# Normalized tokens of 56 tiles: turned by TensorE, or by VectorE and DRAM

## The chip, the core and the metric

The kernel runs on one core of a Trainium2 chip, as one program. A core has a matrix engine (TensorE, PE in the profile, with its weight loads shown apart as PEld), a vector engine (VectorE, DVE), a scalar engine (ScalarE, ACT), a general engine (GpSimd, POOL), and SyncE (SP), which here issues the data transfers. A transfer moves between DRAM and the on-chip memory (SBUF) on 16 DMA engines. TensorE writes its results to a small second memory (PSUM), from which VectorE or ScalarE has to carry them to SBUF. Each engine works through its own list of instructions in order, and waits on semaphores for the others. The metric is the device time of one execution, in microseconds, as the median of several.

## The reference

The input `x` is 2 images of 1024 tokens with 1024 channels, in float32. Four layers follow each other, each with a residual: attention A (32 heads of 32, causal, rotary positions, and ten learned adapter tokens), a feed-forward layer, attention B (8 heads of 16, not causal), and the same feed-forward layer again, with the same weights.

```
x = x + attn_a(layernorm(x), w_attn, w_proj, adapter_wte, gating)
x = x + ffn(layernorm(x), W_base, b_base, W_router, b_router, lora_A, lora_B)
x = x + attn_b(layernorm(x), Wqk_w, Wqk_b, Wv_w, Wv_b, Wo_w, Wo_b)
x = x + ffn(layernorm(x), W_base, b_base, W_router, b_router, lora_A, lora_B)

def ffn(x, ...):
    base = x @ W_base.T + b_base                       # 1024 x 1024
    weights = sparsemax(x @ W_router.T + b_router)     # 8 experts
    h = einsum('bsd,edr->bser', x, lora_A)             # rank 16 each
    return base + einsum('bser,bse,ero->bso', h, weights, lora_B)
```

Each dense layer multiplies normalized tokens by weights and sums over the channels. TensorE sums over the partitions of its operands, so the channels have to lie on the partitions, while a layer norm needs each token's channels together on one partition. Between the two every tile of 128 tokens by 1024 channels has to be turned.

## The kernel before

**Tiles.** A tile is 128 tokens; an image has NT = 8. `layernorm` (L241) leaves `xn`, tokens on partitions; `transposed` (L281) turns it by eight 128x128 transposes on TensorE into PSUM, four to a bank, and `evac` (L229) copies each bank to SBUF, by turns on VectorE and ScalarE. The result is `xnT` in attention A (half an image, 512 tokens) and `xt` elsewhere (one tile, eight blocks of 128 channels).

**Order on TensorE.** The attention loop `attend` (L474) writes down TensorE's instructions round by round, and between them a `Filler` (L49) puts in dense work: generators that yield after each matmul what it costs, at 1.7 ns a column. The list is fixed at build time (`manual_schedule`), and TensorE follows it whatever is late. On VectorE and ScalarE the tile framework orders the instructions. SP's list follows the program from the end of stage A on; before that it is the framework's. In the part that the program orders, a transfer's place on SP is where `sp.dma_start` was called.

**Stage A.** Projections of attention A are computed per group of four heads, by a scheme with seven products in place of eight (`seven`, L669), whose combined token blocks `tt` stream from DRAM through five buffers (`Stream`, L613). Image 0 is turned at once (`half`, L730). Image 1 is normalized early (`normalize_ahead`, L736) and put aside in DRAM as `xnd`; `second` (L746) brings it back a tile at a time, and turns it in pieces between the matmuls of group 7 of image 0 and of the first projection of image 1 (`turn_over`, L767). `xnT` has two buffers, so half an image of image 1 can only be placed when that of image 0 is done with.

**The feed-forward layers.** `ffn` (L1243) is called as `f1(0)`, `f1(1)` (first layer, one image each) and four times as `f2` (second layer, half an image each). It goes in pairs of tiles: `hidden` (L1312) computes the router and the low-rank part (`hp`), then come seven products in the order 1, 6, 2, 7, 5, 4, 3 (`seven_added`, L1069), of four matmuls each. Products 6, 7 and 4 use combined weights, which stream from DRAM tile `tf` into one ring (`qkb_f` and `qkb_s` in the profile), four pieces each, issued in `used` as TensorE frees the places: pieces 3 for product 7 as product 6 goes on, pieces 4 for product 4 during product 7, pieces 2 for the next pair. The next pair's tiles are fetched, normalized and turned during the pair; the transposes stand between matmuls (`also`, L1441), as in

```
turns = {(5, 0): (2, 0), (5, 3): (2, 1), (4, 2): (3, 0), (3, 1): (3, 1)}
```

The first pair of the first `f2` goes without the scheme (`plain`, L1342).

**Attention B.** `project_b` (L1470) does a tile at a time: values `bv`, transposes of the next tile, queries and keys `bq`. `project_b(0)` and the first `hp` of `f1(1)` come before the attention loop of B; `f1(1)`, `project_b(1)` and the first `f2` calls are filler inside it. `project_wo` (L1537) adds the output projection `bo` to reloaded tokens `xo`.

`Dense.prepare` (L1690) runs a generator's first steps early, one `yield None` at a time, so that loads and layer norms are under way when its first matmul comes.

## Time and profile before

| | |
|---|---|
| three runs | 2406.2, 2408.8, 2414.7 us |
| median | 2408.8 us |
| span of the profiled execution, first to last instruction | 2407.9 us |
| TensorE busy | 2351.2 us, 98% |
| VectorE, ScalarE, GpSimd busy | 1437.3, 1100.4, 598.6 us |
| moved by DMA | 274.7 MB, the 16 engines 35% busy |

The profiled execution is known by its span; what lies around it isn't shown, and the median of the runs is 0.9 us above the span. Times in the listings are microseconds from the start of the span, unless marked ns. A line of the timeline gives start, length, engine, source line, operation, written tile, read tile, shapes and how many instructions were merged; TensorE's are pipelined, so one instruction's length is more than the time it holds the engine. SPq marks the issue of a transfer on SP. A group's three durations are minimum, median and maximum in ns. A line of the transfers ends with the size and the median time from issue to landing. A stage's line gives the length, then busy time and count of PE, PEld, DVE, ACT and POOL, the granted TensorE clock, the DMA share and GB/s.

By stage: attention A with its projections fills 0 to 1190 us; the output projection of A reaches 1460; `f1(0)` stands alone from 1460 to 1592 and `project_b(0)` to 1645; then the loop of attention B runs to about 2250, and the last two `f2` calls stand alone to the end.

### The profile page before, as it was taken

Reading aid. Unit: us, or ns where it says so; the run is one execution under the profiler, and the core shown is the slowest. Engines: PE = TensorE matmul, PEld = TensorE weight load, DVE = VectorE, ACT = ScalarE, POOL = GpSimd, SP = SyncE. Lnnn points to the kernel's source line nnn. Section 1 sums busy time; section 2 is a strip of 40 time slices with the busy share of each in tenths; the row PEclk is TensorE's granted clock in tenths of the full one; section 3 lists DMA queues with packets and bytes.
Section 4 is the critical chain, followed back from the end, with each engine's and each line's share of the span. In section 5 each row is a group of like instructions: output and inputs, shape, how many; then the busy total and the mean of one; then the engine's idle time right before and its main releaser. Section 6 shows DMA issues by size and latency. Waiting matters only on the chain.

```text
span 2407.9 us, 60616 instructions
## 1 busy us (share of the span) xinstructions
PE 2351.2 (98%) x25151; PEld 1077.8 (45%) x25151; DVE 1437.3 (60%) x4317; ACT 1100.4 (46%) x2106; POOL 598.6 (25%) x933
## 2 busy tenths in 40 slices
PE   8999999999999999999999999999999999999999
PEld 4435443455354444445433445575333653233454
DVE  6587666666656666666651246566666765664453
ACT  3346665666565666666652001012455546564100
POOL 1432232222323232223211114202111111122332
PEclk9999999999999999999999999999999999999999
DMA  4443433333243333332312575441332302323543
GB/s 151 141 132 111 136 91 132 98 94 107 90 123 103 92 96 106 88 98 77 133 58 71 174 258 174 159 148 60 121 94 91 112 20 80 105 85 101 175 158 122
DMA packets 174772, 274.70 MB, mean 114 GB/s; under 512 B 16416, under 2 KB 76960, under 8 KB 174496
## 3 DMA queue, kind: packets, MB, share of 16 engines
q1 hardware_dynamic: 174496, 270.83, 35.2%
q8 instruction: 197, 3.23, 0.6%
q14 instruction: 79, 0.65, 0.1%
HBM read 215.19 MB, written 55.57 MB: 112 GB/s over the span
## 4 chain that ended last, share of the span: by engine, by line
PE 89%; DVE 6%; ACT 2%; DMA 1%; issue 1%; POOL 0%; SPq 0%; DVEq 0%; POOLq 0%; ACTq 0%
PE st L411 10%; PE sc L339 8%; PE y_A L433 5%; PE y L200 5%; PE y_f L198 4%; PE z_f L198 4%; PE z L200 4%; PE st L409 3%; PE x_f L198 3%; PE x L200 3%; PE y_v L200 3%; PE y_f L200 3%; PE y_B L433 2%; PE x_f L200 2%; PE y_p L198 2%; DVE pr_A L352 2%
## 5 line engine op out<-in xcount | busy, mean ns | idle before, releaser
L523 ACT ACTIVATE pt<-st 128x1024 f32<-128x1024 f32 (+1 forms) x418 | 425.5, 1018 | 605.8 <-PE st L411 463.6
L360 ACT ACTIVATE pr_A<-pr_A,nmax_A 128x896 f32<-128x896 f32 (+7 forms) x512 | 389.9, 765 | 55.1 <-DVE nmax_A L352 54.5
L352 DVE CUSTOM_DVE_ANT_0 pr_A<-sc,mask 128x512 f32<-128x512 f32 (+3 forms) x512 | 251.2, 537 | 190.2 <-PE st L411 90.7
L339 PE MATMUL sc<-kT,qT 32*128 32x512 f32 (+3 forms) x1536 | 326.1, 521 | 4.8 <-POOL qT L851 3.0
L411 PE MATMUL st<-qT,kT 32*128 32x512 f32 (+3 forms) x1536 | 306.4, 486 | 0.0
L352 DVE CUSTOM_DVE_ANT_0 pr_A<-sc,mask,part_A 128x512 f32<-128x512 f32 (+1 forms) x256 | 156.2, 647 | 145.7 <-PE sc L339 95.0
L418 POOL TENSOR_SCALAR_AFFINE_SELECT pt<-pt 128x256 f32<-128x256 f32 x256 | 105.9, 431 | 469.1 <-ACT pt L523 469.1
L239 POOL TENSOR_TENSOR xf<-xf,b_base 128x256 f32<-128x256 f32 x100 | 74.5, 775 | 417.8 <-DVE xn_f L267 261.9
L360 ACT ACTIVATE pr_B<-pr_B,nmax_B 128x1024 f32<-128x1024 f32 x128 | 145.5, 1141 | 36.4 <-DVE nmax_B L352 36.3
L433 PE MATMUL y_A<-pt,v 128*32 128x512 f32 (+3 forms) x1536 | 157.9, 498 | 0.0
L339 PE MATMUL sc<-kq,qk 32*128 32x512 f32 x512 | 146.5, 649 | 4.6 <-DVE nmax_B L352 3.8
L411 PE MATMUL st<-rows_B,kq 32*128 32x512 f32 x512 | 145.8, 646 | 2.4 <-ACT pt L523 1.7
L411 PEld LDWEIGHTS st<-qT,kT 32*128 32x128 f32 x1536 | 133.6, 185 | 16.3 <-issue 11.3
L409 PE MATMUL st<-rows_A,ones 3*128 3x512 bf16 (+3 forms) x768 | 127.8, 329 | 5.6 <-DVE nmax_A L352 5.0
L352 DVE CUSTOM_DVE_ANT_0 pr_B<-sc,zeros,part_B 128x512 f32<-128x512 f32 x128 | 91.0, 747 | 59.3 <-PE sc L339 59.3
L409 PEld LDWEIGHTS <-ones 3*128 3x128 bf16 x768 | 36.9, 91 | 194.7 <-issue 187.3
L339 PEld LDWEIGHTS sc<-kT,qT 32*128 32x128 f32 x1536 | 113.0, 184 | 18.3 <-POOL qT L851 5.0
L352 DVE CUSTOM_DVE_ANT_0 pr_B<-sc,zeros 128x512 f32<-128x512 f32 x128 | 83.2, 687 | 60.4 <-PE sc L339 60.2
L850 POOL TENSOR_TENSOR qr<-qr,sin 128x256 f32<-128x256 f32 x64 | 61.3, 957 | 220.9 <-DVE qr L846 213.9
L360 ACT ACTIVATION_READ_ACCUMULATOR pr_A<-pr_A,nmax_A 128x1 f32 x512 | 97.2, 190 | 0.0
L200 PE MATMUL y<-tt,wqk 128*32 128x512 f32 x768 | 92.6, 594 | 0.0
L433 PEld LDWEIGHTS y_A<-pt,v 128*32 128x32 f32 x1536 | 33.7, 108 | 118.2 <-issue 109.9
(424 smaller groups left out, 4232.8 us busy)
## 6 DMA issues: line engine op xcount, KB each, us to landing
tt<-td SPq DMA_DIRECT2D x252, 256.0 KB, 2.9
qkb_f<-tf SPq DMA_DIRECT2D x96, 256.0 KB, 3.0
qkb_s<-tf SPq DMA_DIRECT2D x84, 256.0 KB, 2.9
wqk<-in_w_attnT SPq DMA_DIRECT2D x32, 512.0 KB, 5.2
xf<-x SPq DMA_DIRECT2D x25, 512.0 KB, 3.7
xa<-in_x SPq DMA_DIRECT2D x16, 512.0 KB, 6.0
wv<-in_w_attnT SPq DMA_DIRECT2D x8, 1024.0 KB, 5.3
yd<-ys SPq DMA_DIRECT2D x32, 256.0 KB, 2.7
```

Of the source, the lines that this page charges most:

```text
L198: return pe.matmul(out, lhsT=lhsT, rhs=rhs, start=start, stop=stop, skip_group_check=True)
L200: pe.matmul(out[i : i + 32], lhsT=lhsT[:, i : i + 32], rhs=rhs, start=start, stop=stop, skip_group_check=True)
L239: pool.tensor_add(dst[:, i : i + 2 * P], a[:, i : i + 2 * P], b[:, i : i + 2 * P])
L339: yield w * COL, lambda: pe.matmul(dst[:, o : o + w], lhsT=self.qt[rows, qc : qc + P], rhs=self.kt[rows, c0 : c0 + w], start=True, stop=True)
L352: minimum[0] = dve.tensor_tensor_reduce(pr[:, c0 : c0 + w], sc[:, i, o : o + w], m, -self.scale, BIG if c0 == 0 else self.part[:, col], AL ...
L360: tc.keep_in_program_order(act.activation(pr[:, :nk], pr[:, :nk], AF.Exp, bias=self.nmax[:, col], scale=-1.0, accum_out=self.sums[:, col]))
L409: yield w * COL / 4, lambda: pe.matmul(dst[:, o : o + w], lhsT=of["ones"][three, :], rhs=self.rows[three, off : off + w], start=True, stop ...
L411: yield w * COL, lambda: pe.matmul(dst[:, o : o + w], lhsT=self.kt[rows, kb * P : (kb + 1) * P], rhs=rhs, start=self.extra, stop=True)
L418: pool.affine_select(out=dg, in_=dg, compare_op=ALU.is_ge, fill=0.0, base=0, pattern=[[0, 2], [1, P]], channel_multiplier=-1)
L433: pe.matmul(self.y[32 * h : 32 * h + 32, off : off + w], lhsT=self.value(h, kb), rhs=pt[h // 2][:, h % 2, o : o + w], start=self.opens, st ...
L523: act.activation(pt[:, :, low_:wide_], st[:, :, low_:wide_], AF.Exp, scale=ts[0][0].scale)
L850: pool.tensor_mul(qr[:, hs], qr[:, hs], sin[:, cols][:, hs])
```

## The change

All 56 tiles that went through TensorE on the dense stages' way, save image 0's eight in stage A, are turned otherwise: eight of image 1 in stage A, 32 in the feed-forward layers, 16 in `project_b`. A normalized tile is turned by one VectorE instruction in blocks of 32x32 (each block in its place), written to a DRAM tile, and read back by 16 transfers, one for each pair of 32 tokens and 32 of the partitions, in runs of 32 floats (128 bytes). The 16 reads land in the places that the evictions of PSUM wrote.

```diff
+    def turned_out(pl, tag, xn, dst, name, bufs=None):
+        d = pl.tile([P, 4, NC, 32], F32, tag=tag, name=f"d_{name}", **({"bufs": bufs} if bufs else {}))
+        pin(dve.transpose(d.rearrange("p b c i -> p c b i"), xn.rearrange("p (c b i) -> p c b i", b=4, i=32)))
+        sp.dma_start(dst, d.rearrange("p b c i -> p (b c i)"))
+
+    def turned_in(dst, src):
+        rows = src.rearrange("(a j) (b c i) -> a b j c i", a=4, b=4, i=32)
+        for b in range(4):
+            for a in range(4):
+                sp.dma_start(dst[32 * b : 32 * b + 32, :, 32 * a : 32 * a + 32], rows[a, b])
...
-                    sp.dma_start(xnd[t - 1], xn)
+                    turned_out(big, "t4k", xn, xnd[t - 1], f"a1_{t - 1}")
...
+        def second(n):
+            xnT[1, n] = big.tile([P, NC, HF], F32, tag="h16", name=f"xnT1_{n}")
+            for i in range(4):
+                turned_in(xnT[1, n][:, :, i * P : (i + 1) * P], xnd[4 * n + i])
...
+                    if (b, g, i) == (0, NG - 1, 13):
+                        second(0)
```

The second half, `second(1)`, is read at the start of image 1's first projection. In `ffn` the write follows the layer norm, and the reads are issued at set products:

```diff
         def normalize(i):
...
+            def rest():
+                pool_add(xs[t], xs[t], w["b_base"])
+                turned_out(wk, "xd", xns.pop(t), xd, nm, 2)
...
-            turns = {(5, 0): (2, 0), (5, 3): (2, 1), (4, 2): (3, 0), (3, 1): (3, 1)}
             def ready(i):
...
-                if not last and i in (6, 7):
-                    normalize(2 * p + 2 + (i == 7))
+                if not last and i in (6, 2):
+                    normalize(2 * p + 2 + (i == 2))
+                if not last and i in (5, 3):
+                    turn(2 * p + 2 + (i == 3))
```

`xt` has three buffers in place of two. At the start of a call both first tiles are normalized in one step of `prepare` and read in the next. In `project_b` the reads of tile t + 2 are issued ahead of tile t's matmuls, and tile t + 3 is normalized after its values:

```diff
+            if t + 2 < NT:
+                turn(t + 2)
             cols = slice(t * P, (t + 1) * P)
             vp = next_bank([P, P], f"bv{b}_{t}")
...
-            if t + 1 < NT:
-                settle(f"b{b}_{t + 1}")
-                yield from transposed(*ready[t + 1], f"b{b}_{t + 1}", by=(bank, next_bank))
-            if t + 2 < NT:
-                normalize(t + 2)
+            if t + 3 < NT:
+                normalize(t + 3)
```

The program is built with a smaller scratch area for transfers issued by GpSimd (`dynamic_dma_scratch_size=1024`), which leaves SBUF for the new tiles.

More of the change, by code (lines that the diff above doesn't have):

```diff
@@ L564, in tile_model, with turning @@
     xnd = [dram.tile([P, C], F32, name=f"xnd{t}") for t in range(NT)]
+    turns = [0]
+    def turning():
+        turns[0] += 1
+        return dram.tile([P, C], F32, name=f"xtd{turns[0]}")
     def stage_a(wk, big):
@@ L744, in normalize_ahead @@
                 yield ("norm", t)
-        def second():
-            def load(t):
-                xn = big.tile([P, C], F32, tag="t4k", name=f"xn1_{t}")
-                sp.dma_start(xn, xnd[t])
-                return xn
-            xns = {t: load(t) for t in range(2)}
-            for t in range(NT):
-                n, i = divmod(t, 4)
-                if i == 0:
-                    yield None
-                    xnT[1, n] = big.tile([P, NC, HF], F32, tag="h16", name=f"xnT1_{n}")
-                if t + 2 < NT:
-                    xns[t + 2] = load(t + 2)
-                yield from transposed(xns.pop(t), xnT[1, n][:, :, i * P : (i + 1) * P], f"a1_{t}")
-        given = [False]
-        owed = [0]
-        def turn_over():
-            owed[0] += 1
-            if given[0]:
-                given[0] = False
-                return
-            while owed[0]:
-                owed[0] -= 1
-                yield next(turnover)
+        def second(n):
+            xnT[1, n] = big.tile([P, NC, HF], F32, tag="h16", name=f"xnT1_{n}")
+            for i in range(4):
+                turned_in(xnT[1, n][:, :, i * P : (i + 1) * P], xnd[4 * n + i])
         def adapter_scores(u):
-            given[0] = True
             b, g, n = u.at
@@ L809, in late @@
             spent = 0.0
-            given[0] = False
             for u, at in begun.items():
@@ L883, in project_first @@
             else:
-                assert next(turnover) is None
+                second(1)
                 yield from begin_values(b, 0)
@@ L897, in project_first @@
                         yield HF * COL
-                        if b and n == 0 and c % 2:
-                            yield from turn_over()
                     rotate(b, 0, key, n, qp)
@@ L902, in project_first @@
                         yield adapter_keys(0)
-                if b and n == 0:
-                    while owed[0]:
-                        owed[0] -= 1
-                        yield next(turnover)
                 yield ("qk", b, 0, n)
@@ L914, in project_blocks @@
             k, q = st["k", b, g], st["q", b, g]
-            if (b, g) == (0, NG - 1):
-                assert next(turnover) is None
             halves = {i: (t, n) for i, t, n in ((11, k, 0), (12, k, 1), (21, q, 0), (22, q, 1))}
@@ L938, in project_blocks @@
                         yield adapter_keys(g)
-                    if (b, g) == (0, NG - 1) and i > 12 and i % 2 == 0:
-                        yield from turn_over()
-            while owed[0]:
-                owed[0] -= 1
-                yield next(turnover)
+                    if (b, g, i) == (0, NG - 1, 13):
+                        second(0)
             yield ("qk", b, g, 1)
@@ L1042, in stage_a @@
         ahead = normalize_ahead()
-        turnover = second()
         for b in range(B):
@@ L1250, in ffn @@
         seq = [t for p in range(0, len(tiles), 2) for t in (tiles[p + 1], tiles[p])]
-        xs, xns, xts, hws, stores = {}, {}, {}, {}, deque()
+        xs, xns, xts, hws, stores, places_of = {}, {}, {}, {}, deque(), {}
         room = kept[2 if k else b]
@@ L1260, in normalize, with place, turn @@
             t = seq[i]
-            xns[t] = layernorm(wk, "xn", xs[t], f"f{b}_{k}_{t}", behind=True,
-                               then=lambda: pool_add(xs[t], xs[t], w["b_base"]))
-        def turn(i, parts=(0, 1), by=None):
-            t = seq[i]
-            settle(f"f{b}_{k}_{t}")
-            return transposed(xns[t], place_xt(i) if 0 in parts else xts[t], f"f{b}_{k}_{t}", parts, by)
-        def place_xt(i):
-            t = seq[i]
-            xts[t] = room["xt"] if room and i % 3 == 2 else wk.tile([P, NC, P], F32, tag="xt", name=f"xt_f{b}_{k}_{t}", bufs=2)
-            return xts[t]
+            nm = f"f{b}_{k}_{t}"
+            xd = turning()
+            def rest():
+                pool_add(xs[t], xs[t], w["b_base"])
+                turned_out(wk, "xd", xns.pop(t), xd, nm, 2)
+            def place():
+                xts[t] = room["xt"] if room and i % 4 == 3 else wk.tile([P, NC, P], F32, tag="xt", name=f"xt_{nm}", bufs=3)
+                turned_in(xts[t], xd)
+            xns[t] = layernorm(wk, "xn", xs[t], nm, behind=True, then=rest)
+            places_of[i] = place
+        def turn(i):
+            settle(f"f{b}_{k}_{seq[i]}")
+            places_of.pop(i)()
         def store(t, n):
@@ L1360, in plain @@
                     if (i, n, c) == (1, 0, 1):
+                        turn(2)
                         while stores:
@@ L1365, in plain @@
                         normalize(3)
-                    if i and c == 5:
-                        yield from turn(2, (1 - n,))
                     if (i, n, c) == (0, 1, 5):
@@ L1375, in plain @@
                     yield HF * COL
-            settle(f"f{b}_{k}_{seq[3]}")
-            yield from transposed(xns[seq[3]], place_xt(3), f"f{b}_{k}_{seq[3]}", by=(next_bank, next_bank))
+            turn(3)
         def take_room():
@@ L1391, in ffn @@
         normalize(0)
+        normalize(1)
         yield None
-        normalize(1)
+        turn(0)
+        turn(1)
         yield READY
@@ L1396, in ffn @@
             take_room()
-        for i in range(2):
-            yield from turn(i, by=(bank, next_bank))
         n_pairs = len(tiles) // 2
@@ L1437, in ready @@
                     fill.flush("wb1")
-                if not last and i in (6, 7):
-                    normalize(2 * p + 2 + (i == 7))
+                if not last and i in (6, 2):
+                    normalize(2 * p + 2 + (i == 2))
+                if not last and i in (5, 3):
+                    turn(2 * p + 2 + (i == 3))
             def also(i, k, dst):
-                if not last and (i, k) in turns:
-                    j, part = turns[i, k]
-                    yield from turn(2 * p + j, (part,))
                 if (i, k) == (2, 1):
@@ L1470, in project_b @@
     def project_b(b, w, fk, wk, st):
-        xs, ready = {}, {}
+        xs, xts, xds = {}, {}, {}
         def fetch(t):
@@ L1477, in normalize, with turn @@
         def normalize(t):
-            xn = layernorm(fk, "xn", xs.pop(t), f"b{b}_{t}", behind=True)
-            ready[t] = xn, fk.tile([P, NC, P], F32, tag="xt", name=f"xt_b{b}_{t}", bufs=2)
+            xds[t] = turning()
+            xn = layernorm(fk, "xn", xs.pop(t), f"b{b}_{t}", behind=True,
+                           then=lambda: turned_out(fk, "xd", xn, xds[t], f"b{b}_{t}", 2))
+        def turn(t):
+            settle(f"b{b}_{t}")
+            xts[t] = fk.tile([P, NC, P], F32, tag="xt", name=f"xt_b{b}_{t}", bufs=3)
+            turned_in(xts[t], xds.pop(t))
         fetch(0)
@@ L1484, in project_b @@
         normalize(0)
+        normalize(1)
+        fetch(2)
+        yield None
+        turn(0)
+        turn(1)
         yield READY
+        normalize(2)
+        fetch(3)
         qk = st["qk", b] = wk.tile([P, 2, T], F32, tag=f"qkb{b}", name=f"qk{b}", bufs=1)
@@ L1490, in project_b @@
         pool.memset(vm, 0.0)
-        normalize(1)
-        fetch(2)
-        fetch(3)
-        settle(f"b{b}_0")
-        yield from transposed(*ready[0], f"b{b}_0", by=(bank, next_bank))
+        fetch(4)
         for t in range(NT):
-            xnT = ready.pop(t)[1]
+            xnT = xts.pop(t)
             if t >= NT - 2:
                 yield AHEAD
+            if t + 2 < NT:
+                turn(t + 2)
             cols = slice(t * P, (t + 1) * P)
@@ L1514, in project_b @@
                 yield AHEAD
-            if t + 1 < NT:
-                settle(f"b{b}_{t + 1}")
-                yield from transposed(*ready[t + 1], f"b{b}_{t + 1}", by=(bank, next_bank))
-            if t + 2 < NT:
-                normalize(t + 2)
-            if t + 4 < NT:
-                fetch(t + 4)
+            if t + 3 < NT:
+                normalize(t + 3)
+            if t + 5 < NT:
+                fetch(t + 5)
             qp = next_bank([P, 2, P], f"bq{b}_{t}")
@@ L1759 @@
     arrays = {f"in_{k}": np.ascontiguousarray(v) for k, v in arrays.items()}
-    nc = bacc.Bacc("TRN2", target_bir_lowering=False, num_devices=1)
+    nc = bacc.Bacc("TRN2", target_bir_lowering=False, num_devices=1, dynamic_dma_scratch_size=1024)
     d = {
```

## The prediction

> **What bounds the kernel now.** I read the page first, then the groups of the operations that change, then TensorE and SP in order of time around each place where tiles are turned. First the page:

> ```profile
> span 2407.9 us, 60616 instructions
> PE 2351.2 (98%) x25151; PEld 1077.8 (45%) x25151; DVE 1437.3 (60%) x4317; ACT 1100.4 (46%) x2106; POOL 598.6 (25%) x933
> ...
> PE 89%; DVE 6%; ACT 2%; DMA 1%; issue 1%; POOL 0%; SPq 0%; DVEq 0%; POOLq 0%; ACTq 0%
> ```

> TensorE (PE) is the bound nearly everywhere, in an order fixed at build time: a TensorE instruction whose operand is late holds back all behind it, attention too. Work taken from TensorE is a gain, and so is every microsecond of lateness a loss. Next, TensorE inside a dense pair, and the two groups of transposes:

> ```profile
> 1475.54 3.60 PE L198 MATMUL y_f<-qkb_f,xt_f 128*128 128x512 f32 x8
> ...
> 1479.83 0.60 PE L204 MATMUL xt_f<-ident,xn_f 128*128 128x128 f32 x4
> 1480.27 2.74 PE L198 MATMUL z_f<-wb,kqb_f 128*128 128x512 f32 x6
> ...
> 1484.14 2.74 PE L198 MATMUL y_f<-qkb_f,xt_f 128*128 128x512 f32 x6
> ```
> ```profile
> L204 PE MATMUL xt_f<-ident,xn_f x256: 272/273/330, 1458.2 to 2369.8; 128*128 128x128 f32 x128
> ...
> L204 PE MATMUL xt_b<-ident,xn_b x128: 272/273/330, 1591.3 to 1934.4; 128*128 128x128 f32 x128
> ```

> One transpose shows 0.27 us, but they are pipelined: from 1479.83 to 1480.27 four of them hold TensorE for 0.44 us. That is the price removed. Now SP, which issues every transfer, in order:

> ```profile
> 1405.59 8.59 SPq L1135 DMA_DIRECT2D yt<-yd  x16
> ...
> 1468.64 10.84 SPq L1281 DMA_DIRECT2D qkb_f<-tf  x8
> ...
> 1592.58 18.40 SPq L1475 DMA_DIRECT2D xb<-x  x6
> ```
> ```profile
> qkb_f<-tf SPq DMA_DIRECT2D x96, 256.0 KB, 3.0
> ...
> yt<-yd SPq DMA_DIRECT2D x128, 64.0 KB, 2.1
> ...
> xnd<-xn_a SPq DMA_DIRECT2D x8, 512.0 KB, 3.0
> ...
> adT<-in_adT SPq DMA_DIRECT2D x1, 128.0 KB, 7.5
> ```

> Sixteen small reads in a row occupy SP for 8.59 us, 0.54 each, and land 2.1 us after issue. That is the nearest row to the 16 reads of a turned tile: 8.6 us of SP, and 10.7 from first issue to usable. The `qkb_f` line is the stream of combined weights: each piece is issued when TensorE frees its place, just ahead of use. SP has slack now, but not 8.6 us at that spot. Last, two stages and the clock:

> ```profile
> 1492.70:1525.90 33.20, 33.20 (x116) 17.62 (x115) 18.86 (x56) 3.12 (x9) 10.19 (x14) 1.00 0.48 159
> ...
> 1592.00:1648.00 56.00, 53.35 (x466) 51.72 (x464) 41.84 (x148) 9.03 (x26) 5.55 (x8) 1.00 0.36 118
> ```
> ```profile
> 295.00:300.00 5.00, 3.28 (x26) 1.73 (x24) 3.89 (x15) 3.34 (x9) 0.88 (x1) 1.00 0.80 261
> 300.00:303.50 3.50, 3.50 (x38) 0.78 (x35) 1.47 (x8) 2.22 (x6) 0.77 (x2) 0.58 0.32 114
> ```

> A dense pair of `f1(0)` takes 33.2 us with TensorE never idle; `project_b(0)` takes 56 us, 7 a tile. In the last two rows TensorE idled 1.72 us, and the granted clock was then 0.58 for 3.5 us: a stall costs another 3.5 x 0.42 = 1.5 us.

> **The change, part by part.** *Removed:* 56 tiles x 8 transposes, 112 x 0.44 = 49.3 us of TensorE, and 112 evictions, half on ACT (0.585 us), half on DVE (0.69), together 33 and 39 us; and 8 reads `xn<-xnd`. *Added:* 56 DVE transposes of 128x1024. No such row exists; the nearest are the shuffles, 0.294 us for 128 columns and 0.726 for 512, so 1.13 ns a column and 1.30 us for 1024 (the plain 1024-column normalization, 0.81, is the low end, two 512 shuffles, 1.45, the high). 73 us on DVE, minus 39: +34 on an engine 60% busy, beside TensorE; I take 0, at most 34 if its cover is gone. The wait for several read semaphores ahead of each tile is left at 0 too (the 21 semaphore events on the weight queue took 0.05 us; eight a tile, 56 tiles, 23 us as the high end, hardly below nothing). *SP:* 56 x 17 - 16 = 936 more issues x 0.54 = 503 us, through one queue that also carries the weight pieces, activations and stores. The smaller POOL scratch costs nothing: no POOL-issued queue is in the trace.

> Whether the 503 us are hidden depends on where they stand in SP's order in the changed program. I take the places in turn, net of the transposes removed there.

> *(a) Stage A, image 1.* The halves are now fetched by 64 reads in one go, 64 x 0.54 = 34.6 us. The first go follows product 2 of group 7 (ends 544.3) and stands ahead of `tt` pieces 4_1 to 4_3, which product 4 uses at 563.7 now, 561.7 without transposes. Reads end at 578.9, the piece lands 2.9 later: a stall of 16 to 20, I take 18. The second go starts at 598.5 and is ready at 635; its first use (637.4 now) moves to 630 to 634: +3. Gain: 8 x 0.88 = 7.0, and 3.6 of waits for evictions. Two clock dips. Sum +13.4.

> *(b) Start of `f1(0)`.* Normalized tiles at 1449.3 and about 1452, transposed and written by 1453, first write landed (3.0) at 1453.5, 32 reads to 1471, landed 1473. `hp_f` of the second tile ran at 1462.3: +10.7, and a dip, +12.2.

> *(c) Its pairs.* With product 6 at 0: the first turned tile's write now precedes weight pieces 3 and leaves at 6.1 (normalized at 4.9, transpose 1.3), so product 7 starts at 9.4 instead of 7.95 and, its last pieces standing behind the second write, ends at 13.7 instead of 11.4. Then 16 reads run 10.1 to 18.7 ahead of pieces 4, which land at 21.6; product 5 and its low-rank part are done at 18.0. Product 4 stalls 3.6 us. The next `hp_f` waits for the second tile's reads until 32.3, and the period is 37.6 for 33.15: +4.45, and a dip, for three turning pairs: +17.9. If DVE finished both transposes before product 6 ended, 2.3 less a pair.

> *(d) `project_b(0)`, the largest.* SP's order per tile is: load, write, then at once the 16 reads of that same tile. So SP waits for its own write to land, and a tile costs 0.5 + 3.0 + 8.6 = about 12.4 us, against 5.1 of TensorE work. Tiles 0 and 1 are turned ahead (landed 1590.8 and 1599.4), tile 2 lands at 1613.9, tile 7 at 1676, and TensorE ends near 1680 for 1646. The first two tiles of `f1(1)` stand behind all this: load 3.7, normalize and transpose 5.6, write 3.0, 32 reads 17.3, landing 2.1, so hidden work ends at 1707.8 for 1652: +55, +56.5 with a dip. TensorE's order puts `hp_f` before attention, so nothing covers it.

> *(e) `f1(1)`.* A pair takes 50 us here and product 7 comes late enough; pieces 4 land at 1729.2 where 1729.7 is due. No stall: -1.76 x 3 = -5.3.

> *(f) `project_b(1)` and the first `f2`.* SP 12.4 a tile against 10.3: 3 late at most from this. But `xo` loads of `project_wo` now stand behind reads; `bo` of tile 3, 1918.6 now, waits until about 1936, and then 32 reads after its store end near 1958 where `hp_f` stood at 1945.8: +13. The end of the plain pair waits for one tile's reads: +6.

> *(g) Last three `f2`.* One hidden turn: -1.8. Start of (1,0): 32 reads from 2257, landing 2276.4, and `xo_7` behind them: +6. Its turning pair +6.0. Start of (1,1): landing 2344.6 for 2339.4 plus 1.85: +3.4 and a dip; its pair +6.0. Together +21.1.

> **Sum:** 13.4 + 12.2 + 17.9 + 56.5 - 5.3 + 13 + 6 + 21.1 = +134.8 on the span of 2407.9: 2542.7. The three runs' median, 2408.8, is 0.9 above the span (they spread 8.5): 2544.

> [...] The row on the clock says 1.72 us of idleness cost 1.5. [...] And the row of sixteen small reads says SP's issue is the limit, not the bytes. [...] I go by the rows.

> **Rivals.** *Gain:* SP issues the reads quickly and all turns hide; then -49, 2360. It is decided by the spacing: counting (a) 128, (b) 32, (c) 48, (d) 128, (f) 64, (g) 96, some 496 issues lie on the path, so break-even is 0.54 - 134.8 / 496 = 0.27 us. The shortest issue in the trace is 0.319; for it speaks only that no 32-partition read was seen. 4%. *Cheaper queue:* 0.43 us, the bare instruction, and no dips (ten counted, 15 us): 2544 - 55 - 15 = 2474. For it: `tf` pieces follow each other at 0.46. 18%. *The transfers bind:* 128-byte runs were seen once, `adT`, 1024 runs landing in 7.5 us; less 2.1 and times four that is 21.6 us a tile for 8.6, and 31 tiles x 13 = +403, 2947. Against: it queued behind four 512 KB loads; its own packets are 13 ns each in the trace's records and all started within 1.85 us, 7.4 a tile, under SP's 8.6. At 0.8 us a read: 2673. 13%. That the change isn't what it says is ruled out by the changed program's order.

> **How the numbers follow.** My sum has 64%, its own range 2490 to 2600 (spacing 0.46 to 0.6, DVE's 34 and the semaphores' 23 partly felt). The 8-in-10 range reaches to the cheaper queue and half into the slow transfers: 2470 to 2640. Within 0.3% is what this kernel's runs can't tell from no change: 1%. Faster 4%, slower 95%.

> **What would show it.** After: no L204 group on `xn`; SP rows of x16 and x64 reads at 0.5 us; TensorE idle until `DMA xt_b`, `xt_f` and `tt` in the waits; `project_b(0)` near 90 us; a 37 us pair period; clock dips. Wrong if reads are spaced under 0.4 us, if a read takes over 1 us, or if TensorE's idle time lies elsewhere.

## The result

The changed kernel takes 2651.5 us (median of four runs, 2647.9 to 2655.0), the kernel before beside it 2409.6: ratio 1.1006, 95% interval 1.0981 to 1.1030. That is 242 us slower. Forecast were 135, with a range up to 2640: the sign and most of the places were right, the size was too small by 107 us.

From the page of the profile after, and below it the row PEclk of the page before:

```profile
PE 2408.7 (91%) x25597; PEld 1073.4 (40%) x25597; DVE 1465.3 (55%) x4317; ACT 1070.5 (40%) x2050; POOL 598.4 (23%) x933
...
PEclk9999999989999999999999889878898899999899
...
PE 65%; DVE 11%; SPq 10%; DMA 9%; issue 3%; ACT 1%; POOL 0%; DVEq 0%; POOLq 0%; ACTq 0%
```
```profile
PEclk9999999999999999999999999999999999999999
```

In the chain that ends last TensorE fell from 89% to 65%, and SP's issues (SPq) came in with 10% where they had none. But TensorE's busy time did not fall by the 49 us of transposes, it rose by 57.5: the row PEclk, the granted clock in tenths, has 8s and a 7 where the row of before has 9s alone. TensorE not only waits, it also works slower: the granted clock is 0.75 in `project_b(0)` and 0.86 in the pairs of `f1(0)`, where it was 1.00 before (last tables of this section). The waits themselves, in the view of waits:

```profile
PE hp_f L198 <- DMA xt_f<-xtd: 38.8, 8, 14.4
PE bv L198 <- DMA xt_b<-xtd: 34.1, 7, 9.0
PE y_f L198 <- DMA qkb_f<-tf: 20.6, 11, 5.1
PE y L200 <- DMA tt<-td: 19.2, 1, 19.2
PE y_f L198 <- DMA qkb_s<-tf: 11.2, 7, 3.7
```

The columns after the names are total, times and longest. There are two kinds of waits: for the turned tiles themselves (`xt_f`, `xt_b`), 72.9 us in these rows, and for other transfers that stand behind them on SP, the weight pieces (`qkb_f`, `qkb_s`) and the combined token blocks (`tt`), 51.0 us.

The groups of the new instructions, and two transfers from the view of transfers (last column: median us from issue to landing):

```profile
L304 DVE STREAM_TRANSPOSE d_f<-xn_f 128x1024 f32<-128x1024 f32 x32 | 39.6, 1238 | 0.5
```
```profile
xt_f<-xtd SPq DMA_DIRECT2D x400, 32.0 KB, 1.9
...
out<-xf SPq DMA_DIRECT2D x26, 256.0 KB, 4.5
```

VectorE's turning takes 1.24 us (1.30 forecast), a small read lands 1.9 us after issue (2.1 forecast). The stores `out<-xf`, which the change does not touch, land 4.5 us after issue where they took 2.2: many of them travel behind the small reads (with one whole read in place of sixteen, experiment 2, they take 3.0).

Last, stages that answer to the table of windows. Columns: window, its length, busy time of PE, PEld, DVE, ACT, POOL, granted clock, DMA share, GB/s. The stages are: stage A; the three turning pairs of `f1(0)`; its last pair; `project_b(0)` up to the first `hp_f` of `f1(1)`; `f1(1)`; `project_b(1)`.

```profile
0.00:1224.90 1224.90, 1164.54 (x16672) 545.91 (x16673) 771.57 (x2378) 697.16 (x1424) 344.25 (x573) 0.98 0.36 107
...
1511.70:1645.30 133.60, 109.64 (x295) 51.88 (x294) 57.06 (x179) 5.60 (x21) 30.63 (x42) 0.86 0.57 160
1645.30:1674.60 29.30, 26.01 (x59) 10.07 (x58) 17.54 (x37) 2.24 (x9) 4.63 (x6) 1.00 0.63 189
1674.60:1784.80 110.20, 61.73 (x385) 60.45 (x385) 44.94 (x137) 2.84 (x14) 5.64 (x8) 0.75 0.48 117
1784.80:2012.60 227.80, 211.49 (x1764) 69.11 (x1768) 138.07 (x415) 83.96 (x143) 35.35 (x48) 0.93 0.46 130
2012.60:2135.30 122.70, 98.26 (x1789) 58.98 (x1782) 76.90 (x224) 45.09 (x77) 18.64 (x25) 0.86 0.52 139
```

The same stages before, without the last pair of `f1(0)`:

```profile
0.00:1193.50 1193.50, 1160.78 (x16549) 551.45 (x16550) 767.42 (x2378) 700.73 (x1431) 345.06 (x573) 1.00 0.36 110
...
1467.60:1567.00 99.40, 99.40 (x343) 52.86 (x342) 55.84 (x163) 9.35 (x27) 31.05 (x42) 1.00 0.49 159
...
1592.60:1647.40 54.80, 52.39 (x457) 50.99 (x458) 41.07 (x146) 8.14 (x25) 5.55 (x8) 1.00 0.36 121
1647.40:1853.00 205.60, 205.30 (x1800) 71.14 (x1799) 135.52 (x417) 95.25 (x161) 35.00 (x48) 1.00 0.29 92
1853.00:1945.80 92.80, 87.77 (x1356) 60.83 (x1357) 73.64 (x222) 42.25 (x76) 19.35 (x25) 0.96 0.29 101
```

Set against the same places before, with idle time as length less PE's busy time, and lost clock as busy time times (1 - granted clock), summed over windows of 1 us:

| step of the prediction | forecast | measured | of it idle | of it lost clock |
|---|---|---|---|---|
| (a) stage A | +13.4 | +31.4 | +27.6 | +10.6 |
| (b) end of the projection of A, start of `f1(0)` | +12.2 | +12.7 | +10.0 | +4.6 |
| (c) pairs of `f1(0)` | +17.9 | +37.9 | +27.0 | +13.2 |
| (d) `project_b(0)`, first `hp_f` of `f1(1)` | +56.5 | +55.4 | +46.1 | +17.8 |
| (e) `f1(1)` | -5.3 | +22.2 | +16.0 | +14.1 |
| (f) `project_b(1)`, to the first `hp_f` of `f2` | +13 | +29.9 | +19.4 | +8.3 |
| (f), (g) the `f2` calls | +27.1 | +55.9 | +41.8 | +18.8 |
| sum | +134.8 | +245.4 | +187.9 | +87.4 |

The two right columns and the 49 us of transposes do not quite add up: 19 us of busy time, mostly in `project_b(1)` and `f2`, belong to neither, and where they come from stays open. The recorded sum held some 15 us of clock (ten dips) and, with the 49 taken off, about 169 of idle time. So of the 110 us that are missing, 73 are clock, 19 idle time, and 19 that rest. This sorts the time and does not yet say what lengthened the kernel: in step (d) 16 us more of lost clock than forecast did not make the step longer.

### The profile page after: what moved, and what is told of

It is laid out like the page before. It is cut to its first block, busy times and chain, and to the rows that moved or that the text cites. A ratio compares the mean times of both kernels' runs of the same rounds, so it can differ in the third digit from the quotient of the medians.

```text
span 2653.3 us, 62732 instructions
## 1 busy us (share of the span) xinstructions
PE 2408.7 (91%) x25597; PEld 1073.4 (40%) x25597; DVE 1465.3 (55%) x4317; ACT 1070.5 (40%) x2050; POOL 598.4 (23%) x933
## 4 chain that ended last, share of the span: by engine, by line
PE 65%; DVE 11%; SPq 10%; DMA 9%; issue 3%; ACT 1%; POOL 0%; DVEq 0%; POOLq 0%; ACTq 0%
SPq L313 9%; PE st L426 8%; PE sc L354 7%; PE y_A L448 5%; PE y L200 5%; PE z L200 3%; PE st L424 3%; PE x L200 3%; PE y_v L200 2%; PE y_f L200 2%; PE y_B L448 2%; PE y_f L198 2%; DMA xf<-x 2%; PE y_p L198 2%; PE z_f L198 2%
## 5 line engine op out<-in xcount | busy, mean ns | idle before, releaser
L354 PE MATMUL sc<-kq,qk 32*128 32x512 f32 x512 | 149.3, 660 | 13.7 <-DVE nmax_B L367 10.4
L354 PEld LDWEIGHTS sc<-kT,qT 32*128 32x128 f32 x1536 | 114.0, 185 | 27.1 <-DVE part_A L367 11.2
L200 PE MATMUL y<-tt,wqk 128*32 128x512 f32 x808 | 98.7, 599 | 19.2 <-DMA tt<-td 19.2
L200 PE MATMUL x<-xnT,wqk 128*32 128x512 f32 x688 | 85.3, 607 | 0.0
## 6 DMA issues: line engine op xcount, KB each, us to landing
tt<-td SPq DMA_DIRECT2D x252, 256.0 KB, 2.8
qkb_f<-tf SPq DMA_DIRECT2D x96, 256.0 KB, 3.5
qkb_s<-tf SPq DMA_DIRECT2D x84, 256.0 KB, 3.3
wqk<-in_w_attnT SPq DMA_DIRECT2D x32, 512.0 KB, 5.1
xtd<-d_f SPq DMA_DIRECT2D x32, 512.0 KB, 2.9
xf<-x SPq DMA_DIRECT2D x25, 512.0 KB, 3.7
xa<-in_x SPq DMA_DIRECT2D x16, 512.0 KB, 5.3
```

Of the source, the lines that this page charges most:

```text
L200: pe.matmul(out[i : i + 32], lhsT=lhsT[:, i : i + 32], rhs=rhs, start=start, stop=stop, skip_group_check=True)
L354: yield w * COL, lambda: pe.matmul(dst[:, o : o + w], lhsT=self.qt[rows, qc : qc + P], rhs=self.kt[rows, c0 : c0 + w], start=True, stop=True)
```

## The experiments

Ratios are to the kernel before on the same chip (2411 to 2414 us). Stages are read from each kernel's own trace, as in the table.

**1. The parts one by one.** Three kernels, each the kernel before with one part of the change: stage A alone, the feed-forward layers alone, `project_b` alone.

> Only the eight tiles of stage A, image 1, are turned by VectorE and DRAM; the dense layers and project_b keep TensorE's transposes. The recorded step (a) is +13.4 us on 2409.6, so 2423. The table of stages of the two traces says +31.4 at the end of stage A, of which 10.6 is lost clock: 2441 if nothing of it is given back. Rival (the parts disturb each other): under 2420, with the rest appearing only when all three parts are changed.

> Only the tiles of the dense layers (f1 and f2) are turned by VectorE and DRAM; project_b keeps TensorE's transposes, with three buffers in place of two for its turned tiles. The recorded steps are (b) 12.2, (c) 17.9, (e) -5.3, the first hp_f of f1(1) of (d) about 28, of (f) about 6 to 13, and (g) 21.1: +80 to +87, so 2490 to 2497. The table of stages says 12.7 + 37.9 + 22.2 + 12.5 + 43.4 and some 20 of the 55 at the end of project_b(0): +149, so 2559. Rival (parts disturb each other): near 2490.

> Only the sixteen tiles of project_b are turned by VectorE and DRAM. The recorded steps (d) without the first hp_f of f1(1) and (f) without f2: +28 and +3, so 2441. The table of stages: some 35 of the 55 of project_b(0) and 20 to 30 of project_b(1): +55 to +65, so 2465 to 2475. If the three parts add up, the three differences of this call sum to 242; if they disturb each other, to much less.

Measured: 2437.8 (+26.5; 1.0108, 1.0078 to 1.0137), 2533.9 (+122.6; 1.0506, 1.0468 to 1.0545), 2483.4 (+72.1; 1.0297, 1.0267 to 1.0327). They sum to +221 of 242. Each is a loss by itself, and most of the whole is their sum; the 21 us that are left are a little more than the intervals of the four differences allow together (some 15), and were not followed up.

One number in these traces was not expected. Stage A of the last two kernels is the same as before, and yet takes 1200.5 and 1201.0 us where the profiled execution of before took 1193.5, all by lost clock (11.5 for 3.3). So some 7 us of step (a) are luck of the profiled execution, not of the change. (The runs of the kernel before spread likewise: 2405.3 us at a granted clock of 0.996 to 2417.8 at 0.991.)

In the trace of the changed kernel stage A also has 9.4 us of waits of attention for its softmax (`sc` for `part_A` on VectorE, twice, the longest 5.4 us), against 1.7 before. Each time VectorE had stood still shortly before, 2.2 us for a load `xa` and 4.1 us for a load `wv`, with the softmax behind it in its list. With the stall for `tt` and the lucky 7 us that is most of what step (a) has above its forecast; the sum had no such wait.

**2. What about the reads costs the time?** First the number of issues. The short runs move to the write, and the read comes back whole:

```diff
-        sp.dma_start(dst, d.rearrange("p b c i -> p (b c i)"))
+        flat = dst.rearrange("p f -> (p f)").rearrange("(j m a i) -> a j m i", j=32, m=32, a=4)
+        for a in range(4):
+            sp.dma_start(flat[a], d[32 * a : 32 * a + 32].rearrange("p b c i -> p (b c) i"))
...
+        sp.dma_start(dst.rearrange("p c q -> p (c q)"), src.rearrange("p f -> (p f)").rearrange("(j b f) -> b j f", j=32, b=4))
```

> Same turning, same blocks, same 128-byte runs, but they are put on the write: each turned tile goes to DRAM in 4 writes whose runs are 128 bytes, and comes back in 1 read of runs of 4 KB (4 reads of 512-byte runs in stage A): 5 issues on SyncE's queue for 17. Theory 1 (the number of issues ahead of others in SyncE's order): 56 tiles save 12 issues of 0.5 us, the small-read bursts of 8 us become 2.5; the stalls at qkb_f and tt nearly go, the wait of SyncE for its own write stays; project_b(0) near 70 us; in all 2430 to 2470. Theory 2 (the 128-byte runs themselves are slow, wherever they stand): the writes take 5 us or more to land, 2580 to 2650. Theory 3 (VectorE's turning delays softmax and evictions): no change, 2640 or more.

Measured 2663.0 (1.1042, 1.1007 to 1.1076): no gain at all from 12 issues fewer a tile. Theory 1, as the number of issues alone, falls. The total alone would suit theory 3 (VectorE); experiment 4 tests that one, and the trace shows what holds SP. SP in `project_b(0)` of this kernel:

```profile
1702.93 9.32 SPq L307 DMA_DIRECT2D xtd<-d_b  x4
1714.85 0.56 SPq L317 DMA_DIRECT2D xt_b<-xtd  x1
1715.45 8.14 SPq L307 DMA_DIRECT2D xtd<-d_b  x4
```

Four writes hold SP for 8.1 to 9.3 us, as long as sixteen reads did. The same place in the changed kernel:

```profile
1704.79 7.89 SPq L313 DMA_DIRECT2D xt_b<-xtd  x16
1712.72 0.45 SPq L1459 DMA_DIRECT2D xb<-x  x1
1713.59 0.34 SPq L305 DMA_DIRECT2D xtd<-d_b  x1
1718.13 7.72 SPq L313 DMA_DIRECT2D xt_b<-xtd  x16
```

Either way 4096 runs of 128 bytes a tile take 7.7 to 9.3 us here. In the pairs of `f1(0)` the four writes hold SP for only 3.0 us, and yet the three pairs take 143.2 us for 133.6: these 3 us now stand ahead of the weight pieces of product 7. Why the same writes take two to three times as long in `project_b(0)` is not shown. Only in stage A, where the writes are made long before anybody needs them, did the edit help: 1200.0 for 1224.9.

Then the runs. Sixteen reads of eight whole rows each, which leave the blocks where they are:

```diff
...
+        rows = src.rearrange("p (c q) -> p c q", c=NC)
+        for k in range(16):
+            sp.dma_start(dst[8 * k : 8 * k + 8], rows[8 * k : 8 * k + 8])
```

> Sixteen reads a tile as before, at the same places of SyncE's order, but of eight whole rows each, in long runs and not in 128-byte runs; the blocks are not put in their places, so the values are others. Theory 1 (number of issues): nothing changes, 2620 to 2660, reads spaced 0.5 us. Theory 2 (the 128-byte runs): the reads land sooner and disturb the weight stream less: under 2560.

Measured 2589.9 (1.0733, 1.0701 to 1.0764). Both theories missed: the number of issues matters after all once the runs are long, but less time is lost. SP again:

```profile
1717.20 5.34 SPq L312 DMA_DIRECT2D xt_b<-xtd  x16
```

With long runs sixteen reads hold SP for 5.34 us, 0.33 each; with 128-byte runs it was 0.49 in the changed kernel. (In stage A, where a row is cut into eight pieces of 512 bytes, 64 such reads took 44.4 us, 0.69 each, and that stage grew to 1250.5. These have 64 runs each and are slower than those with 256 runs of 128 bytes, so the number of runs alone does not give the time.)

At last one whole read in place of sixteen, the blocks again left where they are:

```diff
...
+        sp.dma_start(dst, src.rearrange("p (c q) -> p c q", c=NC))
```

> Each turned tile comes back in one read of whole rows in place of sixteen of 128-byte runs; the blocks are not put in their places, so the values are others. Neither the number of issues nor short runs are left, only VectorE's turning, the write, its landing and the read, at the same places of the order. Theory 1 (the time that SyncE is held by the reads is the main cost): what is left is the round trip, 3.0 + 3.3 us, exposed at the start of each dense layer and at each tile of project_b: project_b(0) 65 to 75 us, f1(0)'s pairs near 33 us each, 2420 to 2470. Rival (the round trip and the order are most of it): 2520 or more. Third (all hidden): below 2411, by up to 49 us.

Measured 2460.3 (1.0197, 1.0159 to 1.0235): theory 1 in its second form, the time for which the reads hold SP. Stage A is back at 1196.4, `project_b(0)` at 58.9 for 54.8, the `f2` calls at 462.1, as before. Outside stage A, which is out of line in the middle one, the three traces take 1261, 1339 and 1428 us with SP held for 0.45, 5.34 and 7.8 us a tile: the first 4.9 us a tile cost 78 us, the next 2.5 cost 90. So the loss is not in proportion to the time for which SP is held. That would fit slack which covers part of the first microseconds and none of the last; it was not tested further. Pairs of `f1(0)` (119.1 us for 99.5) and `f1(1)` (218.9 for 205.6) did not come back; that is taken up in 3.

The wait of SP for its own write, taken away by reading a tile that was written long before:

```diff
-                turned_in(xts[t], xd)
+                turned_in(xts[t], xnd[t])
...
-            turned_in(xts[t], xds.pop(t))
+            turned_in(xts[t], xnd[t])
```

> The tiles of the dense layers and of project_b are still turned and written, but the sixteen reads of each fetch a tile that was written in stage A, long before, so that SyncE never waits for its own write; the dense layers compute on other values. By step (d), 3.0 of the 12.4 us that a tile of project_b takes on SyncE is that wait: its period falls from 13.3 to about 10, some 25 us for project_b(0); 16 tiles of f1(0) starts and pairs lose 2 to 3 us each: in all 40 to 70 us less, 2580 to 2610. Rival (the write's landing is hidden): no change within 1 per cent. Rival (the landing is all of it): under 2500.

Measured 2620.0 (1.0857, 1.0826 to 1.0889): 31 us less, below the 40 to 70 expected. `project_b(0)` gains 17 us and `project_b(1)` 13, in the pairs of `f1(0)` it is 4. Here the landing counted where SP stands still for it, and elsewhere hardly.

**3. What the order on SP does.** The same work is now issued elsewhere or in another order. First the reads of `f1(0)` and `project_b(0)` on ScalarE's queue:

```diff
-                turned_in(xts[t], xd)
+                turned_in(xts[t], xd, act if (b, k) == (0, 0) else None)
...
-            turned_in(xts[t], xds.pop(t))
+            turned_in(xts[t], xds.pop(t), None if b else act)
```

> The sixteen reads of the tiles of f1(0) and project_b(0) are issued on ScalarE's queue, where ScalarE has almost nothing else to do in these two stages; all else as in the changed kernel. Theory 1 (the reads block weight pieces, loads and stores on SyncE): the pair period of f1(0) falls from 45 to 33 to 36 us, the three pairs give back 27 to 34 us; project_b(0) goes from 110 to about 85 to 95, since its reads still take 8 us a tile but writes and loads pass them: 2595 to 2610. Theory 2 (transfers or latency of the turned tile itself): pair period stays at 43 to 45.

Measured 2613.2 (1.0829, 1.0797 to 1.0860). That is just outside the 2595 to 2610 of theory 1. The three pairs of `f1(0)` take 109.9 us for 133.6, `project_b(0)` 96.1 for 110.2. Two of the pairs take 31.9 and 31.6 us, less than the 33.2 before, so there all is hidden; the middle one takes 46.4, with waits of 3.9 us for a weight piece and 4.8 us for its second tile. The reads cost the pairs 24 of their 34 us by standing ahead of other transfers. The start of `f1(0)` became 6 us longer: there the reads run to 1511.7 on ScalarE, to 1502.6 on SP.

Where a pair of the changed kernel loses its time is seen on SP and TensorE, side by side. SP in the second pair of `f1(0)`:

```profile
1555.15 0.32 SPq L1239 DMA_DIRECT2D xf<-x  x1
1555.56 0.38 SPq L1397 DMA_DIRECT2D x<-xf  x1
1559.53 0.32 SPq L1239 DMA_DIRECT2D xf<-x  x1
1564.47 0.32 SPq L305 DMA_DIRECT2D xtd<-d_f  x1
1564.88 1.21 SPq L1270 DMA_DIRECT2D qkb_f<-tf  x2
1570.18 0.32 SPq L305 DMA_DIRECT2D xtd<-d_f  x1
1570.55 1.25 SPq L1270 DMA_DIRECT2D qkb_f<-tf  x2
```
```profile
1555.06 3.60 PE L198 MATMUL y_f<-qkb_f,kqb_f 128*128 128x512 f32 x8
...
1568.17 3.75 PE L198 MATMUL y_f<-qkb_f,xt_f 128*128 128x512 f32 x4 [5.00 <-DMA qkb_f<-tf]
1574.06 3.78 PE L198 MATMUL y_f<-qkb_f,xt_f 128*128 128x512 f32 x4 [2.14 <-DMA qkb_f<-tf]
```

Product 6 starts at 1555.06. The loads of the next tiles leave at +0.1 and +4.5 (in the kernel before at -8.5 and -4.2), so the first write leaves at +9.4 and the second at +15.1, and behind each stand two weight pieces of product 7, which stalls 5.0 and 2.1 us. Four matmuls then take 3.75 us, for 1.88 at full clock.

If the late loads are to blame, stores that are issued ahead of the reads should help:

```diff
                 if not last and i in (5, 3):
+                    while stores:
+                        sp.dma_start(*stores.popleft())
                     turn(2 * p + 2 + (i == 3))
```

> One edit to the changed kernel: in a dense pair, finished halves are stored ahead of the sixteen reads and not behind them, so that the buffers of the next pair's residual tiles come free and their loads leave 6 to 9 us earlier. If the lateness of these loads (and with it of the normalization and of the write that weight pieces 3 stand behind) is what made the pairs of f1(0) 45 us and not 37.6, the period falls to 37 to 40, some 15 to 24 us in f1(0), and something in f2: 2600 to 2635. If not, no change within 0.3 per cent.

Measured 2680.5 (1.1108, 1.1076 to 1.1140), 29 us slower: a miss. In its trace the second pair's writes do leave sooner after product 6 (+5.4 and +10.3), and product 7 stalls 4.4 us for 7.1. But SP waits for VectorE to finish the half that it stores (1540.2 to 1544.6), the second tile's reads leave over 4 us later, and the next `hp_f` waits 5.0 and 4.3 us for them. A wait on SP was exchanged for another.

Writes behind the weight pieces of product 3:

```diff
...
                 if nxt is not None and not (last and nxt == 2 and (k == 0 or end)):
                     piece(nxt, c)
+                if (i, c) == (2, 3):
+                    write()
```

> One edit to the changed kernel: in the dense pairs the write of a turned tile is issued behind the weight pieces of product 3 and not as soon as VectorE is done, so that no weight piece waits for a write that VectorE has not finished. Theory 1 (the stall of product 7 comes from weight pieces that stand behind such a write in SyncE's order): of the 7 us that product 7 loses in each turning pair of f1(0), and the 3 to 4 in f1(1) and f2, most go; against that the reads of the second tile may wait up to 3 us for their write. f1(0)'s three pairs 115 to 122 us for 133.6, f1(1) 215 to 222 for 227.8, in all 2600 to 2630. Rival (VectorE or the loads are what is late, the place of the write means nothing): within 0.5 per cent of 2651.

Measured 2640.4 (1.0944, 1.0902 to 1.0986), 11 us less than the changed kernel (15 by the ratios), about half or less of what was expected: pairs 126.9 for 133.6, `f1(1)` 217.9 for 227.8. Product 7 no longer stalls. But the first tile's reads now start right behind the write's landing, the pieces of product 4 stand behind all sixteen of them, and product 4 waits instead:

```profile
1562.27 3.60 PE L198 MATMUL y_f<-qkb_f,xt_f 128*128 128x512 f32 x8
...
1579.76 6.03 PE L198 MATMUL y_f<-qkb_f,xt_f 128*128 128x512 f32 x8 [9.41 <-DMA qkb_f<-tf]
```

The idle time of the three pairs is even longer, 26.4 us for 24.0. What fell is the lost clock, 5.5 for 13.2: one stall of 9 us a pair in place of two or three short ones.

The same edit where a turned tile comes back in one whole read:

> The kernel with one read of whole rows per turned tile (values are others, no block is put in its place), and besides it the write of a turned tile is issued behind the weight pieces of product 3. With the reads nearly free, f1(0)'s three pairs still took 119 us for 99.5 and f1(1) 219 for 206, each with a stall of 3 us or more in product 7. Theory 1 (weight pieces of product 3 stand behind a write that VectorE has not yet fed): pairs 98 to 105, f1(1) 202 to 210, in all 2425 to 2440. Rival (late loads and VectorE): pairs stay above 115, 2450 to 2465.

Measured 2432.8 (1.0073, 1.0049 to 1.0098). The pairs are at 100.3 (99.5 before) and `f1(1)` at 203.2 (205.6 before, so here a gain). Of the stalls for weight pieces 0.9 us are left in the whole execution; the longest wait is another:

```profile
PE hp_f L198 <- DMA xt_f<-xtd: 12.6, 2, 8.9
```

That settles where 20 and 13 us were: weight pieces behind a write that VectorE has not yet fed. And both edits with the sixteen reads:

> Both edits to the changed kernel with its sixteen reads: the reads of f1(0) and project_b(0) on ScalarE's queue, and the writes of turned tiles of the dense pairs behind the weight pieces of product 3. Theory 1 (nothing but SyncE's order makes f1(0)'s pairs longer): three pairs at 96 to 103 us for 133.6 (109.9 with the first edit alone), in all 2580 to 2600. Rival (the 4096 short runs of a tile also hold up the weight pieces in the transfers, whichever queue issues them): pairs stay at 107 or more.

Measured 2639.7 (1.0932, 1.0895 to 1.0969): a miss, pairs 129.4. The reads of a tile, issued together with the weight stream, now take 8.6 to 14.9 us on ScalarE's queue, and the second `hp_f` of a pair waits 7 to 9 us. The rival's number came out, but not its reason: no weight piece is waited for in these pairs, it is the reads themselves that are late. So with the sixteen reads a pair has no room left: what is taken from one wait comes back in the next. How much of the 8.6 to 14.9 us is the transfers' own rate and how much ScalarE's waits was not separated.

**4. VectorE.** The kernel before, and besides it VectorE turns every normalized tile of the dense layers and `project_b` into a tile that nobody reads:

```diff
+            if tag == "xn":
+                d = pl.tile([P, 4, NC, 32], F32, tag="xd", name=f"d_{name}", bufs=2)
+                pin(dve.transpose(d.rearrange("p b c i -> p c b i"), xn.rearrange("p (c b i) -> p c b i", b=4, i=32)))
```

> The kernel before, with its TensorE transposes, and besides them VectorE turns every normalized tile of the dense layers and of project_b into a tile that nobody reads: 48 x 1.24 = 59 us more on VectorE, nothing else. The prediction took VectorE's work at 0, its high end at 34. Theory 1 (hidden beside TensorE): +0 to +10. Rival (VectorE's turning delays the softmax and the normalizations that TensorE waits for, and is a main part of the 242): +30 or more.

Measured 2426.1 (1.0054, 1.0035 to 1.0072): +12. The two profiled executions differ by 16.0 us, of which 7.2 lie in stage A, where nothing was added: 59 us of VectorE's work cost some 9 at their own places. The eight tiles of stage A are not in this test.

**5. The clock.** Seven stalls in the projection of A of the kernel before:

```diff
...
+                if i == 4:
+                    l4 = left[4].rearrange("p a q -> p (a q)")
+                    dve.scalar_tensor_tensor(l4, halves[22], 0.0, l4, ALU.mult, ALU.add)
+                    for _ in range((0, 1, 2, 4, 6, 9, 14)[4 * b + p - 1]):
+                        dve.tensor_scalar(l4, l4, 1.0, None, ALU.mult)
```

> The kernel before, with seven stalls of known length put in proj_a: ahead of product 4 VectorE rewrites its left factor, value unchanged, once behind product 5 and then 0, 1, 2, 4, 6, 9 and 14 times more, so TensorE waits about 1.7, 2.1, 2.5, 3.2, 4, 5 and 7 us. The prediction's step: each stall costs 1.5 us of clock besides its length, 10.5 in all. [...] Either way +30 to +45 in all.

Measured 2453.0 (1.0167, 1.0119 to 1.0215). The stalls came out as 0.45, 0.98, 2.98, 3.90, 4.82, 7.63 and 12.94 us, and lost, by the windows of 1 us, 0, 0, 1.7, 2.7, 2.2, 2.2 and 1.9 us of clock, 10.7 in all where seven dips of 1.5 make 10.5: the sum fits, the single price does not. Two of the places, right behind a stall of 0.98 and of 4.82 us (same columns as the table of stages):

```profile
1333.50:1337.00 3.50, 3.49 (x32) 1.40 (x36) 0.00 (x0) 0.37 (x2) 0.41 (x1) 1.00 0.28 100
...
1427.10:1432.00 4.90, 4.87 (x7) 2.07 (x8) 0.00 (x0) 0.00 (x0) 0.00 (x0) 0.55 0.03 10
```

The changed kernel's own trace has many more stalls to sort. Five of 0.9 to 1.2 us lost nothing; of 24 between 1.2 and 2.75 half lost nothing, the others 1.5 us or more; 31 longer ones all lost 1.4 to 4.5, most near 1.7 or near 3.

```profile
2487.95:2491.36 3.41, 2.39 (x6) 0.76 (x4) 1.66 (x13) 0.00 (x0) 0.63 (x1) 1.00 0.88 277
2491.36:2494.78 3.42, 1.87 (x5) 0.92 (x6) 1.33 (x2) 0.00 (x0) 2.13 (x4) 1.00 0.65 217
2494.78:2498.19 3.41, 3.41 (x10) 1.50 (x9) 1.70 (x5) 0.99 (x3) 0.00 (x0) 1.00 0.92 287
2604.01:2607.42 3.41, 1.25 (x3) 0.19 (x1) 1.38 (x2) 0.00 (x0) 0.53 (x1) 1.00 0.56 149
2607.42:2610.84 3.42, 3.07 (x4) 1.46 (x5) 0.00 (x0) 0.00 (x0) 0.00 (x0) 0.50 1.02 349
```

These are counts in the traces of this case; what sets the granted clock is not shown.

## Why the prediction was wrong, and where it was right

**Right.** TensorE's fixed order as the bound, and SP as the place where the time is lost; the spacing of reads (0.49 us for 0.54), the landing (1.9 us for 2.1), VectorE's 1.24 us; the stall for `tt` in stage A (19.2 us for 18); steps (b) and (d), the largest of all, each within 1.1 us of its forecast, with tiles of `project_b(0)` at 13.3 us for 12.4. That VectorE's work hides was taken at 0 and measured at about 9, outside stage A. The rivals with a lower total are refuted; "the transfers bind", 2673 at 0.8 us a read, came near in its total, but by a spacing that the trace does not show.

**The term that was mis-sized: "and a dip".** The sum counted ten dips of 1.5 us, 15 in all. The profile after has 39 where before had 6, and they lose 99 us against 12, 2.5 us each. Both factors were too small, the number more so. (The row that gave 1.5 ended 0.45 us before its slow stretch did; the whole stretch of 3.41 us at half clock makes 1.7.) A late transfer was counted as one stall with one dip, but at the start of a layer each of two tiles is waited for, a weight stream stalls product 7 in two places, and every tile of `project_b` stalls anew. Not every dip lengthened the kernel. One dip in step (d) stood for eight in the trace, and the step still came out as forecast: there SP sets the pace, and a slower TensorE only fills time in which it would have waited. Of the 73 us above the forecast, 53 lie in the steps that ran over theirs.

**The step that failed by its mechanism: (c) and, with it, (e).** Both took the layer norms of the next pair to be on time, as before ("normalized at 4.9"), and only shifted what follows. But the loads of those tiles stand behind stores, and these behind the second tile's reads, so the loads left 8.6 us later and the second write at +15.1 us; the weight pieces 3 behind it were what stalled product 7. (c) let those cost 2.3 us, and had product 4 wait 3.6 us a pair and the next `hp_f` after it; (e) took product 7 to come late enough and found no stall. In the trace product 7 waits 20.1 us in the three pairs, product 4 3.1 and `hp_f` 0.7, and a pair takes 43.4 to 45.3 us for the forecast 37.6; in `f1(1)` weight pieces are waited for five times, 8.3 us in all. One whole read together with a later write brings both stages back to 100.3 and 203.2 us. So the time for which the reads hold SP and the place of the write account for the whole of it, but only together: alone, the one read leaves the pairs at 119.1 us and the later write at 126.9. A transfer had been followed to whom it delays, but not on to what that one's data delays.

**Steps (f) and (g)** were low by 17 and 29 us; the clock lost there is 27. The waits in the trace are of the kinds above: in the `f2` calls 18 us for turned tiles and 12 for weight pieces, in `project_b(1)` and its end 11 us of `bo` for its residual tokens and 4 of the first `hp_f`. With one whole read the `f2` calls are back at 462.1 us; what in the order of (f) and (g) was misjudged was not taken apart by a run of its own, and stays open.

**A size that was right by a reason that was not.** The prediction said that SP's issue is the limit and not the bytes. Its spacing came out, but in `project_b(0)` five issues took as long as seventeen, and in all they gained nothing: with runs of 128 bytes the number of issues was not what limited here. With long runs a read takes 0.33 us, hardly more than the shortest issue in the trace of before, 0.32. That the 64 KB reads of another tile gave nearly the right 0.54 is partly luck. In kind the rival on 128-byte runs was nearer, though its 0.8 us was not; whether the short runs are slow in SP's issue or in the transfers behind it was not separated. Joining sixteen 32 KB reads into 128 KB writes gained nothing here while the runs stayed at 128 bytes (2663.0 us for 2651.5).

No version tried beats the kernel before. Even with one read for sixteen, the blocks left in place, and the write in a better position, 19 us are lost.

## What to carry to other kernels

Where one engine runs a fixed list, count the gaps that late operands make one by one, and price each as its length and the clock lost behind it. In the changed kernel's trace each of the 31 gaps over 2.75 us lost 1.4 to 4.5 us of clock, and 12 of the 24 between 1.2 and 2.75 us lost none. Two or three short stalls a pair lost more of it here than one of 9 us (13.2 for 5.5 us in the pairs of `f1(0)`). In `project_b(0)`, where SP sets the pace, 17.8 us more of lost clock left step (d) at +55.4 us for a forecast +56.5. When transfers are put into a queue, follow the chain two links on: not only what stands behind them, but what that one's data feeds, and whether this again holds the queue. Turning through DRAM in runs of 128 bytes held the queue here for some 8 us a tile of 512 KB with 17 issues, and with 5 for 3.0 us in one stage and 6.5 to 10 in another; against 0.88 us of TensorE a tile that needs slack which this kernel does not have.

## What was not expected of the hardware

- A 32 KB read of 256 runs is spaced 0.49 us on SP, one of long runs 0.33 us, one of 64 runs of 512 bytes 0.69 us; four writes of 1024 runs each hold SP for 3.0 us in a pair of `f1(0)` and 6.5 to 10 us in `project_b(0)`, tile after tile.
- Stores that follow such reads land 2 us later here (`x<-xf` 4.1 for 2.1 us, `out<-xf` 4.5 for 2.2), and in the second pair of `f1(0)` the next load `xf<-x` leaves 4.9 us after the store ahead of it (1550.22 to 1555.15) for 2.1 before (1490.15 to 1492.23).
- A stage in which nothing was changed took 1193.5 us in one profiled execution and 1200.5 to 1201.6 in four other kernels. In the two of them that left stage A's part of the change out (the feed-forward layers alone, `project_b` alone) the lost clock was 11.5 us for 3.3. In the trace of the changed kernel, gaps of 1.2 to 2.75 us lost clock in 12 of 24 cases; by the idle time within pieces of 3.413 us, 5 of 14 pieces with 1.3 to 1.9 us, and all 35 with more, were followed by half clock.
